# Layer 0 of a four-layer image kernel: one partial sum kept in a PSUM bank, two additions moved from VectorE to GpSimd

## The chip, the cores and the metric

The kernel runs as one launch on one core of a Trainium2 chip. The metric is the device time of a launch in microseconds (us), the median of the runs shown. The engines are named as the profile names them: PE is TensorE, PEld its weight loads, DVE is VectorE, ACT is ScalarE, POOL is GpSimd, and SP is SyncE, which here only issues DMAs.

## The reference, cut to what matters

The input is a tensor of 2 images x 64 channels x 256 x 256 pixels, float32. Four residual layers follow one another; each normalises its input in groups of channels first. The change touches layer 0 alone:

```python
x = x + layer0(_gn(x), img, w_pos, w_img, w_comp)   # then layers 1 (state-space scan), 2 (patch FFT + conv), 3 (block DCT)

def layer0(inp, ...):
    em = concat([w_img @ resized(img), w_pos @ positions])        # 64 channels
    un_em, un_fea = _unfold3x3(em), _unfold3x3(inp)               # 3x3 neighbours, 2 pixels apart
    feature_score = einsum('bckhw,bchw->bkhw', un_em, em)         # em of the neighbour . em of the pixel
    comp_score = sigmoid(einsum('bckhw,c->bkhw', un_fea, w_comp)) # belongs to the neighbour alone
    return einsum('bckhw,bkhw->bchw', un_fea, comp_score * feature_score)
```

Every pixel gets nine terms: its own and those of eight neighbours. The feature score of two pixels is the same from both ends, so that a kernel has to compute it for four directions only.

## The kernel before, in words

The two images with their 64 channels fill the 128 partitions. Layer 0 works on pairs of rows: a **step** `n` is two rows of 256 pixels, a tile of 128 x 512 float32[...]. There are 128 steps, and blocks of eight rows (`R`, four steps, `per`) are loaded by DMA. The loop variable `t` runs over 133 iterations and skews the work: in iteration `t` the embedding of step `t` is made, the products of step `t-2`, the scores and terms of step `n = t-3`, and the sum and the output of step `last = t-4`. The order of every engine's queue is the order of the program (`manual_schedule` names all five engines)[...].

Per iteration, each engine does this, in this order:

- **PE**, eleven matmuls: `pl` (L318) and `pe` (L320) in `embed`; then `score` (L360) of the square `sq`, `score` A, `out` A (L403), `score` B, `out` C, `score` C, `out` D, `score` D, `out` B. A `score` multiplies a tile of products with a block matrix: it sums the 64 channels of an image and puts the sum on all its partitions, in a bank `pf`. The `out` matmuls multiply with the identity and add the four terms of `last` in the bank `acc`.
- **ACT**: `sg` (sigmoid of `pl`), `e` (two halves, from `pe`), `fea` (normalised rows of step `t+1`), `sq` (L352).
- **POOL**: the addition of B for `last` (L380); four products of `e` with its shifted self (`pr`, L355); `gated`, the tile `g` = `fea` x `sg` (L333).
- **DVE**: `mult` "c" (L365), the pixel's own term, from `g` (SBUF) and `pf` (PSUM) into a tile of SBUF; then for each of the four directions `mult` (the neighbour's `g` times the score, for the pixel) and `move` (L370, the pixel's `g` times the score, for the neighbour, into the padded tiles `mvA` to `mvD`); additions (L380) between them; at last `yt` = `xt` + `acc` (L438) and the statistics of `yt` (L439). SP then issues the store of `yt` (L440).

The directions A, B, C, D are the shifts (0, 2), (2, -2), (2, 0), (2, 2) in rows and columns. `moved_to(n, name)` is the view of a moved tile as the receiving pixel sees it: for A that of the same step, for B, C and D that of the step before. After one step the term A holds A + own + moved A, C holds C + moved C, D holds D + moved D, all three added on DVE, and B + moved B is added on POOL an iteration later.

[...] one each for `pl`, `pe` and `acc`, five for `pf`. `acc` has only one bank, so `out` A of an iteration has to wait until `yt` of the iteration before has read it. `pr` has eight buffers (two steps), `term` ten, `fea`, `sg`, `sq` and `yt` two each.

Of the kernel before, what the change touches and what calls it, by code (L numbers as in the profile page):

```python
# [10 lines left out]
F32 = mybir.dt.float32  # L11
BF16 = mybir.dt.bfloat16
AF = mybir.ActivationFunctionType
ALU = mybir.AluOpType
PSUM = bass.MemoryType.PSUM
DRAM = bass.MemoryType.DRAM

P = 128
# [102 lines left out]
class Kernel:  # L121
# [115 lines left out]
    def layer0(self, x, y, coeffs):  # L237
# [3 lines left out]
        nc, tc, a = self.nc, self.tc, self.a  # L241
# [8 lines left out]
        with ExitStack() as ctx:  # L250
# [39 lines left out]

            p_l = ctx.enter_context(tc.tile_pool(name="l0pl", bufs=1, space=PSUM))
            p_e = ctx.enter_context(tc.tile_pool(name="l0pe", bufs=1, space=PSUM))
            p_f = ctx.enter_context(tc.tile_pool(name="l0pf", bufs=5, space=PSUM))
            p_o = ctx.enter_context(tc.tile_pool(name="l0po", bufs=1, space=PSUM))

            xt, fea, sq, pr, term = {}, {}, {}, {}, {}
            inner = slice(2, 2 + W)

            def load(k):
                if 0 <= k < nblk:  # L300
                    xt[k] = pool.tile([P, R, W], F32, name="xt", bufs=3)
                    nc.sync.dma_start(xt[k], xv[:, R * k : R * k + R])
                    nc.sync.dma_start(rts[k % 2][32:38], rv[:, R * k : R * k + R])

            def features(n):
                k, s = divmod(n, per)
                fea[n] = pool.tile([P, 2, W], F32, name="fea")
                self.affine(fea[n], xt[k][:, 2 * s : 2 * s + 2], coeffs)

            def embed(n):  # L310
                k, s = divmod(n, per)
                g, e = gs[k % 2], es[k % 2]
                rows = slice(4 + 2 * s, 6 + 2 * s)
                if s == 0 and k:
                    for t in (gs, es):
                        nc.scalar.copy(t[k % 2][:, 2:4], t[1 - k % 2][:, R + 2 : R + 4])
                pl = p_l.tile([P, 2, W], F32, name="pl")
                nc.tensor.matmul(pl, wcomp, fea[n], start=True, stop=True)  # L318
                pe = p_e.tile([P, 2, W], F32, name="pe")
                nc.tensor.matmul(  # L320
                    pe, w_e, rts[k % 2][:, 2 * s : 2 * s + 2], start=True, stop=True
                )
                sg = pool.tile([P, 2, W], F32, name="sg")
                nc.scalar.activation(sg, pl, AF.Sigmoid)
                for i in range(2):
                    r = 2 * n + i
                    nc.scalar.activation(
                        e[:, 4 + 2 * s + i, inner],
                        pe[:, i],
                        AF.Identity,  # L330
                        bias=by_row[:, r : r + 1],
                    )
                return lambda: nc.gpsimd.tensor_tensor(  # L333
                    g[:, rows, inner], fea.pop(n), sg, ALU.mult
                )

            def at(n):

                k, s = divmod(n, per)
                if s == per - 1 and k + 1 < nblk:  # L340
                    return gs[(k + 1) % 2], es[(k + 1) % 2], 2
                return gs[k % 2], es[k % 2], 4 + 2 * s

            def near(t, j, name):
                dy, dx = shift[name]
                return t[:, j + dy : j + dy + 2, 2 + dx : 2 + dx + W]

            def products(n):
                _, e, j = at(n)
                own = e[:, j : j + 2, inner]  # L350
                sq[n] = pool.tile([P, 2, W], F32, name="sq")
                nc.scalar.activation(sq[n], own, AF.Square)  # L352
                for name in "ABCD":
                    t = pool.tile([P, 2, W], F32, name="pr", bufs=8)
                    nc.gpsimd.tensor_tensor(t, own, near(e, j, name), ALU.mult)  # L355
                    pr[n, name] = t

            def score(t):
                pf = p_f.tile([P, 2, W], F32, name="pf")
                nc.tensor.matmul(pf, self.block, t, start=True, stop=True)  # L360
                return pf

            def mult(n, name, in_, pf):
                t = pool.tile([P, 2, W], F32, name="term", bufs=10)
                nc.vector.tensor_tensor(t, in_, pf, ALU.mult)  # L365
                term[n, name] = t

            def move(n, name, own, pf):
                t = moved[name][n % len(moved[name])]
                nc.vector.tensor_tensor(t[:, :, inner], own, pf, ALU.mult)  # L370

            def moved_to(n, name):

                dy, dx = shift[name]
                n -= dy // 2
                return moved[name][n % len(moved[name])][:, :, 2 - dx : 2 - dx + W]

            def add(eng, n, name, other):
                t = term[n, name]
                eng.tensor_add(t, t, other)  # L380
# [4 lines left out]
            with tc.manual_schedule(engines={E.PE, E.DVE, E.Activation, E.Pool, E.SP}):  # L385
                features(0)
                for t in range(nstep + 5):
                    if t and t % per == 0:
                        load(t // per + 1)
                    gated = embed(t) if t < nstep else None  # L390
                    if t + 1 < nstep:
                        features(t + 1)

                    n, last = t - 3, t - 4
                    acc = None
                    if 0 <= last < nstep:
                        acc = p_o.tile([P, 2, W], F32, name="acc")
                        if last:
                            add(nc.gpsimd, last, "B", moved_to(last, "B"))

                    def out(name):
                        if acc is not None:
                            nc.tensor.matmul(  # L403
                                acc,
                                self.ident,
                                term.pop((last, name)),
                                start=name == "A",
                                stop=name == "B",
                            )

                    if 0 <= t - 2 < nstep:
                        products(t - 2)
                    if gated:
                        gated()
                    if 0 <= n < nstep:
                        g, _, j = at(n)
                        own = g[:, j : j + 2, inner]
                        pf = score(sq.pop(n))
                        mult(n, "c", own, pf)
                        for i, name in enumerate("ABCD"):  # L420
                            pf = score(pr.pop((n, name)))
                            out("ACDB"[i])
                            mult(n, name, near(g, j, name), pf)
                            if name == "A" or n + 1 < nstep:
                                move(n, name, own, pf)
                            if name == "A":
                                add(nc.vector, n, "A", term.pop((n, "c")))
                            if name == "B":
                                add(nc.vector, n, "A", moved_to(n, "A"))
                            if name in "CD" and n:  # L430
                                add(nc.vector, n, name, moved_to(n, name))
                    else:
                        for name in "ACDB":
                            out(name)
                    if acc is not None:
                        k, s = divmod(last, per)
                        yt = pool.tile([P, 2, W], F32, name="yt")
                        nc.vector.tensor_add(yt, xt[k][:, 2 * s : 2 * s + 2], acc)  # L438
                        nc.vector.bn_stats(stats[:, last, :], yt.rearrange("p r w -> p (r w)"))  # L439
                        nc.sync.dma_start(yv[:, 2 * last : 2 * last + 2], yt)  # L440
# [874 lines left out]
```

## Time and profile before

| | |
|---|---|
| median of 3 runs | 19872.43 us (19870.87 to 19875.25) |
| the profiled execution, its own time | 19870.25 us |
| its span, first to last instruction | 19868.5 us |
| layer 0's loop of steps in the span | about 190 to 1666 us |
| layer 1 with its two scans | about 1676 to 16000 us |
| layers 2 and 3 | from about 16000 us |
| DVE busy, whole span / 300 to 1500 us | 95% / over 99% |
| POOL busy, whole span / 400 to 1400 us | 80% / 71 to 72% |
| one step of layer 0 | 11.45 us |

The times come from the hardware profiler on one execution. Busy is the time in which an engine had at least one instruction under way. Instructions of DVE, POOL and PE are pipelined: the next begins a little before the end of the one before it, so the distance between two starts, and not the duration, is what an instruction costs its queue. A matmul of float32 stands as two records ("x2"). The step time is the distance between the same instruction in two neighbouring steps, for instance `yt` at 909.28 and 920.73 us.

### The profile page before, as it was taken

To read this page: it belongs to the slowest core of one execution; us is meant where nothing else is said; L and a number is where in the kernel's file an instruction comes from. 1 tells how busy PE (TensorE), PEld (TensorE's weight loads), DVE (VectorE), ACT (ScalarE), POOL (GpSimd) and SP (SyncE) were. 2 spreads that over 40 slices of the span, in tenths; PEclk is the share of its full clock that TensorE was granted. 3 is DMA by queue.
4 is the path that set the end of the run, shared out by engine and by line. 5 is a ranking of instruction groups with operands and counts; after the bars stand their busy time and mean duration, and the time that the engine had idled before them with its cause. 6 is when DMAs were issued, how large, how long until landed. Compare 5 with 4: busy or idle time off the path is not lost. (4 is left out here: it accounts for less than half of the span.)

```text
span 19868.5 us, 162340 instructions
## 1 busy us (share of the span) xinstructions
PE 14671.3 (74%) x48720; PEld 4849.2 (24%) x48720; DVE 18868.2 (95%) x16476; ACT 11805.5 (59%) x16810; POOL 15933.1 (80%) x7816
## 2 busy tenths in 40 slices
PE   6886777677767767677677767677777688888886
PEld 3332111111111111111111111111111144444444
DVE  7998999999999999999999999999999989999997
ACT  1224666666666666666666666666666655555554
POOL 4776888888888888888888888888888855555554
PEclk9997666666666666666666666666666689989998
DMA  3114666666666666666666666666666500000003
GB/s 118 47 46 110 152 152 153 151 154 150 155 148 157 147 157 147 157 148 156 149 154 151 153 152 153 152 153 151 152 151 152 136 29 29 29 29 29 29 27 144
DMA packets 662179, 2438.82 MB, mean 123 GB/s; under 512 B 131888, under 2 KB 201264, under 8 KB 450160
## 3 DMA queue, kind: packets, MB, share of 16 engines
q1 hardware_dynamic: 661296, 2428.43, 50.9%
q8 instruction: 385, 6.31, 0.1%
q14 instruction: 498, 4.08, 0.1%
HBM read 1990.14 MB, written 437.78 MB: 122 GB/s over the span
## 5 line engine op out<-in xcount | busy, mean ns | idle before, releaser
L792 DVE TENSOR_TENSOR_SCAN h<-da,st,h 128x512 f32<-128x512 f32 x8192 | 9837.4, 1262 | 309.0 <-ACT da L789 223.8
L796 POOL TENSOR_TENSOR h<-h,cb 128x2048 f32<-128x2048 f32 x2048 | 9255.6, 4519 | 166.0 <-POOL st L795 1.5
L789 ACT ACTIVATE da<-dl,p_a 128x512 f32<-128x512 f32 x8192 | 5564.8, 688 | 3985.3 <-DVE h L792 3892.6
L561 PE MATMUL py<-h,t_c_quad 128*32 128x512 f32 x16384 | 3254.7, 817 | 1656.9 <-POOL h L796 1655.9
L561 PE MATMUL pb<-bc,t_c_sel 64*128 64x512 f32 x3072 | 2696.9, 972 | 2379.9 <-DVE h L773 2374.3
L773 DVE TENSOR_TENSOR h<-dv,pb 128x2048 f32<-128x2048 f32 x1536 | 3470.5, 2259 | 40.2 <-DMA dv<-d_dv 40.2
L1021 POOL TENSOR_TENSOR gl<-gl,prod 128x512 f32<-128x512 f32 x1544 | 1961.1, 1271 | 1493.3 <-ACT prod L1017 1417.9
L755 POOL TENSOR_TENSOR h<-dv,cb 128x2048 f32<-128x2048 f32 x512 | 2319.8, 4531 | 16.3 <-DMA dl<-d_dl 16.3
L980 DVE SCALAR_TENSOR_TENSOR acc<-z,tap_b,acc 128x1024 f32<-128x1024 f32 (+1 forms) x1560 | 1987.3, 1274 | 38.8
L561 PEld LDWEIGHTS pb<-bc,t_c_sel 64*128 64x128 f32 x3072 | 661.0, 267 | 4406.4 <-DVE h L773 4339.5
L795 POOL COPY st<-h 128x4 f32<-128x4 f32 x2048 | 387.3, 189 | 1360.1 <-DVE h L792 1329.1
L561 PEld LDWEIGHTS py<-h,t_c_quad 128*32 128x32 f32 x16384 | 423.8, 122 | 3821.8 <-POOL h L796 3225.7
L561 PE MATMUL mm<-xin,p_conv 64*128 64x512 f32 x4096 | 1321.1, 774 | 15.4 <-DMA x1t<-y 15.4
L1064 PE MATMUL pcv<-z,diag 128*128 128x512 f32 x2322 | 1172.0, 622 | 20.4 <-ACT gl L1072 16.6
L1017 ACT ACTIVATE prod<-z,tap_a 128x512 f32<-128x512 f32 x1544 | 1045.0, 714 | 37.6 <-POOL gl L1021 37.4
L949 ACT COPY z<-pz 128x512 f32<-128x512 f32 x768 | 456.8, 599 | 1027.3 <-PE pz L941 924.8
L941 PE MATMUL pz<-t_c_inv,gf 128*128 128x128 f32 (+1 forms) x8192 | 1038.5, 309 | 1.4 <-ACT z L949 1.0
L941 PEld LDWEIGHTS pz<-t_c_inv,gf 128*128 128x128 f32 (+1 forms) x8192 | 848.3, 181 | 517.4 <-issue 311.9
L561 PE MATMUL mm<-u,p_dt 128*128 128x512 f32 x1024 | 931.3, 1064 | 0.0
L561 PE MATMUL py<-u,p_d 128*128 128x512 f32 x1024 | 820.9, 895 | 0.0
L915 PE MATMUL f<-t_w_inT,xf 64*128 64x384 f32 x2048 | 597.0, 615 | 156.4 <-DVE gf L922 155.5
L561 PEld LDWEIGHTS mm<-xin,p_conv 64*128 64x128 f32 x4096 | 459.7, 244 | 982.5 <-issue 982.3
(166 smaller groups left out, 17767.8 us busy)
## 6 DMA issues: line engine op xcount, KB each, us to landing
cb<-d_bc SPq DMA_DIRECT2D x2048, 320.0 KB
dl<-d_dl SPq DMA_DIRECT2D x2048, 256.0 KB
dv<-d_dv SPq DMA_DIRECT2D x2048, 256.0 KB
d_dl<-delta SPq DMA_DIRECT2D x256, 512.0 KB
d_dv<-du SPq DMA_DIRECT2D x256, 512.0 KB
xin<-in_x SPq DMA_DIRECT2D x16, 2048.0 KB
xt<-in_x SPq DMA_DIRECT2D x32, 1024.0 KB
y<-yt SPq DMA_DIRECT2D x128, 256.0 KB
```

Source lines behind the costliest of these rows:

```text
L561: nc.tensor.matmul(out, lhsT, rhs, start=start, stop=stop)
L755: nc.gpsimd.tensor_tensor(h, t["dv", b], t["cb", b][:, 0].unsqueeze(1).to_broadcast([P, 4, T]), ALU.mult,)
L773: nc.vector.tensor_tensor(h, t["dv", b], pb.unsqueeze(1).to_broadcast([P, 4, T]), ALU.mult)
L789: nc.scalar.activation(da, t["dl", b][:, k], AF.Exp, scale=ws[m]["a"][:, k, j : j + 1])
L792: nc.vector.tensor_tensor_scan(h[:, k], da, h[:, k], state[m, b][:, j, k : k + 1], ALU.mult, ALU.add)
L796: nc.gpsimd.tensor_tensor(h, h, t["cb", b][:, 1 + j].unsqueeze(1).to_broadcast([P, 4, T]), ALU.mult)
L915: nc.tensor.matmul(p, x_f[t][half, g], w_in[half], start=True, stop=True)
L941: nc.tensor.matmul(pz[i * n : (i + 1) * n, k, :, 16 * g : 16 * g + 16], gf[t, 2 * e + g, b][:, c0 : c0 + n], inv, start=True, stop=True,)
L980: eng.scalar_tensor_tensor(out, near(s, name, m0, r, k), w, box["t"], ALU.mult, ALU.add)
L1017: nc.scalar.activation(prod, near(s, name, 4 * h + m, n, k), AF.Copy, scale=w)
L1021: nc.gpsimd.tensor_add(acc, acc, prod)
L1064: nc.tensor.matmul(box["t"], diag[:, k], near(s, f"a{i}", 4 * h + m, n, k), start=k == 0, stop=k == 8,)
```

## The change

The own term "c" goes into a bank `part` of a pool of its own instead of an SBUF tile; the pool for it takes one of the five banks of `pf`. DVE adds the term A to it in place, and then adds moved A to it while writing the term A back to SBUF. The additions of moved C and moved D leave DVE: they stand on POOL at the head of the next iteration, ahead of the addition of B, which has been there already, and so ahead of the products and of `gated`. The number of additions on DVE falls from four to two, and on POOL it rises from one to three.

```diff
-            p_f = ctx.enter_context(tc.tile_pool(name="l0pf", bufs=5, space=PSUM))
+            p_f = ctx.enter_context(tc.tile_pool(name="l0pf", bufs=4, space=PSUM))
+            p_s = ctx.enter_context(tc.tile_pool(name="l0ps", bufs=1, space=PSUM))
...
                         if last:
-                            add(nc.gpsimd, last, "B", moved_to(last, "B"))
+                            for name in "CDB":
+                                add(nc.gpsimd, last, name, moved_to(last, name))
...
                         pf = score(sq.pop(n))
-                        mult(n, "c", own, pf)
+                        part = p_s.tile([P, 2, W], F32, name="part")
+                        nc.vector.tensor_tensor(part, own, pf, ALU.mult)
...
                             if name == "A":
-                                add(nc.vector, n, "A", term.pop((n, "c")))
-                            if name == "B":
-                                add(nc.vector, n, "A", moved_to(n, "A"))
-                            if name in "CD" and n:
-                                add(nc.vector, n, name, moved_to(n, name))
+                                nc.vector.tensor_add(part, term[n, name], part)
+                                nc.vector.tensor_add(term[n, name], moved_to(n, name), part)
```

## The prediction, made before the changed kernel had run

> **What bounds the kernel now.** I read the table of stretches first, since the change touches only the first 1,670 us. Columns: length, then busy us of PE, PEld, DVE, ACT, POOL, granted PE clock, DMA share, GB/s.
>
> ```profile
> 300.00:400.00 100.00, 87.92 (x193) 34.34 (x193) 99.69 (x133) 25.62 (x48) 70.72 (x52) 1.00 0.16 57
> ```
>
> DVE has no idle time, PE lacks 12%, POOL 29%. Then the waits from 300 to 1500 us (total, times, longest): who stands still, and for whom?
>
> ```profile
> POOL term L380 <- PE pf L360: 340.6, 105, 3.3
> ...
> PE acc L403 <- DVE yt L438: 139.9, 105, 1.4
> ```
>
> PE waits for DVE once a step, 1.34 us, with `out` A: the only bank `acc` is free when `yt` has read it. POOL is idle 3.25 us a step, ahead of its addition of B; that starts just after DVE's `mult` B of the iteration before ends, so POOL runs one iteration ahead of DVE. DVE is the bound. Its timeline of one step shows what fills it (start, duration):
>
> ```profile
> 902.14 0.68 DVE L370 TENSOR_TENSOR mvB<-g,pf 128x512 f32<-128x512 f32 x1
> 902.74 1.38 DVE L380 TENSOR_TENSOR term<-term,mvA 128x512 f32<-128x512 f32 x1
> 904.04 0.67 DVE L365 TENSOR_TENSOR term<-g,pf 128x512 f32<-128x512 f32 x1
> ...
> 905.24 1.38 DVE L380 TENSOR_TENSOR term<-term,mvC 128x512 f32<-128x512 f32 x1
> 906.54 0.67 DVE L365 TENSOR_TENSOR term<-g,pf 128x512 f32<-128x512 f32 x1
> ...
> 907.74 1.62 DVE L380 TENSOR_TENSOR term<-term,mvD 128x512 f32<-128x512 f32 x1
> 909.28 0.67 DVE L438 TENSOR_TENSOR yt<-xt,acc 128x512 f32<-128x512 f32 x1
> 909.99 0.69 DVE L439 BATCH_NORM_STATS2 stats<-yt 128x6 f32<-128x512 f32 x1
> ```
>
> From start to start an instruction with one input in PSUM takes 0.60. The additions of moved A, C and D, both inputs in SBUF, take 1.30, 1.30 and 1.54. `yt` to the statistics that read it: 0.71, so a result read by the very next instruction costs 0.11 more. POOL at the same time:
>
> ```profile
> 902.30 1.27 POOL L380 TENSOR_TENSOR term<-term,mvB 128x512 f32<-128x512 f32 x1 [3.25 <-PE pf L360]
> 903.53 5.29 POOL L355 TENSOR_TENSOR pr<-e 128x512 f32<-128x512 f32 x4
> 908.78 1.72 POOL L333 TENSOR_TENSOR g<-fea,sg 128x512 f32<-128x512 f32 x1
> ```
>
> The slow additions meet POOL's instructions. At the loop's end POOL has nothing to do, and the same additions cost what the others do, 1650.28 to 1650.88:
>
> ```profile
> 1650.28 0.68 DVE L380 TENSOR_TENSOR term<-term,mvD 128x512 f32<-128x512 f32 x1
> 1650.88 0.67 DVE L438 TENSOR_TENSOR yt<-xt,acc 128x512 f32<-128x512 f32 x1
> ```
>
> [...]
>
> **The change, part by part** (us a step).
>
> DVE before: 5 `mult` and 4 `move` at 0.60 = 5.40; additions 0.60 + 1.30 + 1.30 + 1.54 = 4.74; `yt` 0.71; statistics 0.61. Sum 11.46; the trace has 11.45 (`yt` at 909.28 and 920.73).
>
> DVE after: the additions of C and D go (-2.84). The other two get `part` from PSUM, so that each has one SBUF input [...]: A + own 0.60, then + moved A 0.71, since it reads the result next to it. Sum 5.40 + 1.31 + 0.71 + 0.61 = 8.03. No row shows DVE writing a full tile to PSUM. Three instructions do it or read it back. Bounds: a cheaper write gains nothing, since DVE will no longer set the pace; at the dear end I let each cost as much as a contended addition, 0.70 more: 8.03 + 2.10 = 10.13. I take 0.60: [...] the trace has 0.67 to 0.68 as duration whether an input lies in SBUF or PSUM.
>
> POOL after: three additions at 1.23 (902.30 to 903.53, uncontended) = 3.69. The four products take 5.25 now because two of them wait for DVE; in the fill of the pipeline, with DVE idle, four took 4.32 (191.72 to 196.04) and `g` 1.23. Sum 9.24, against 8.2 plus 3.25 idle. The added wait: D at the head of POOL's queue needs DVE's `mult` D, and behind it are queued B, the products and `g`. C can start when `mult` C ends; PE's scores C and D are 1.72 apart, C itself takes 1.23, so D waits about 0.3: 9.5 in all. No DMA is issued by the moved work, and SP's queue is unchanged.
>
> PE after: the same eleven matmuls. What do they cost when nothing holds them? The fourth iteration, ahead of the first `yt`, shows it:
>
> ```profile
> 207.30 1.02 PE L318 MATMUL pl<-fea,wcomp 128*128 128x512 f32 x2
> 208.26 1.12 PE L320 MATMUL pe<-rt,w_e 38*128 38x512 f32 x2
> ...
> 216.28 1.02 PE L403 MATMUL acc<-term,t_c_ident 128*128 128x512 f32 x2
> 217.14 1.02 PE L318 MATMUL pl<-fea,wcomp 128*128 128x512 f32 x2
> ```
>
> 9.84 from `pl` to `pl`. (Now: 9.84 + 1.34 stall + about 0.27 for the restart = 11.45.) `out` C and `out` D now wait for POOL instead of DVE; `out` B does so already and still starts 0.86 after its neighbour, so a wait that is fulfilled costs nothing.
>
> So the longest queue is PE with **9.84**, then POOL 9.5, DVE 8.03. Do the waits let PE run through? Take iteration t with `pl` at 0; then, with starts 0.86 apart and the spacings 0.96, 1.05 and 0.96 of the first three, `score` A comes at 3.0, `out` A at 3.8, `out` C at 5.6, `score` C at 6.4, `score` D at 8.1, `out` B at 9.0, ready 10.1 (a matmul's result follows its start by 1.02 and a handover of 0.1). DVE: `mult` C ends about 8.6, `mult` D runs 9.3 to 9.9, `move` D to 10.5, `yt` 10.5 to 11.2. `out` A of t+1 is due at 9.84 + 3.8 = 13.6: 2.4 spare. POOL's C runs 8.6 to 9.9, and `out` C of t+1 is due at 15.4: 5.5 spare. The products end at about 17 and are first read in t+2 at 22.7: 5.7 spare. Four banks `pf`: each score takes the bank of four scores earlier; the tightest, `score` D of t+1 at 18.0, needs `mult` "c" of t+1, done at 13.8: 4.2 spare. So I cost the lost bank and PE's new waits at nothing; with that cover gone, each would cost what its wait exceeds it by.
>
> Saving: 11.45 - 9.84 = 1.61 a step. From `pl` at 217.14 to the last `pl` (t = 127) are 122 distances: 196; the first of them took 12.49 instead of 11.45: 1 more. In the last iterations without `pl` and `pe` PE needs less and DVE sets the pace, 8.03 for 11.44 and 10.29, and about 3 in the last: 9. Sum **206**. The profiled execution had 19870.25, 2.2 under the median and so the same within the spread: 19664 from it, 19666 from the median. I take 19665.
>
> **The rivals.**
>
> 1. *DVE or POOL sets the pace at about 10.1 to 10.5.* Place: the three instructions on `part` (10.13, above), or POOL still held back as now: the products and `g` lose 5.25 + 1.72 - 0.45 (the overlap at `g`'s end) - 5.55 = about 1.0 a step to DVE today, which on top of 9.5 gives 10.5. Against it: no DVE instruction of the loop has two SBUF inputs any more. Time: 1.32 to 0.95 saved on some 125 steps, 165 to 119: 19705 to 19751.
>
> 2. *PE's clock falls, and the kernel is slower.* PE would be busy 99% instead of 88% beside a POOL at 95%. With clock c a step is 9.84/c; from c = 0.86 on this is over 11.45. [...] Against it: [...] the clock is 1.00 throughout this loop, the step at 207 to 217 included. For it: from 16000 us on, with PE busy 87%, the clock is only 0.90; that would give 10.93 and still gain 65.
>
> 3. *The change does not do what it says:* PE stays tied to DVE by a wait I have not seen, and the step stays 11.4: no change, 19870.
>
> **How the numbers follow.** PE-paced as worked out: 0.67, 19650 to 19690. Rival 1: 0.20. Rival 3 and small gains: 0.04. Rival 2 and whatever else holds POOL's head so long that the step passes 11.45: 0.09. A measurement of this kernel tells about 0.2%, 40 us, from no change. Faster by more 0.87, within 0.04, slower 0.09. The range takes the first case and most of rival 1: 19645 to 19750.
>
> **What would show it.** Right: `yt` to `yt` at 9.84 between 300 and 1500 us; PE over 98% busy with no wait of `out` A; DVE idle about 1.8 a step, waiting for PE; additions on DVE at 0.68 duration; POOL about 95% busy, `pr` at 1.1 and `g` at 1.27 without the long forms. PE waiting for POOL in `out` C, or DVE durations near 1.3, mean rival 1. A clock under 0.95 in the loop means rival 2. A step over 10.6 makes the prediction wrong.

## The result: 1.0% faster, and the profile after

The changed kernel takes 19667.11 us (median of 4 runs, 19665.71 to 19668.06) against 19873.76 us of the kernel before beside it (the three runs above and one more). The ratio is 0.9896, with a 95% interval from 0.9881 to 0.9911; 206.7 us are saved. The forecast was 19665 us, a saving of 206.

The span of the profiled execution went from 19868.5 to 19665.9 us. Layer 0's loop, from the first own term on DVE to the last statistics, took 1462.4 us before (203.34 to 1665.72) and takes 1253.3 us now (204.53 to 1457.84): 209.1 less. It starts 1.2 us later, and the layers after it took 5.3 us longer in this execution, in code that the change does not touch. So all of the gain lies in the loop.

The same stretch of the changed kernel (length, then busy us of PE, PEld, DVE, ACT, POOL, granted PE clock, DMA share, GB/s):

```profile
300.00:400.00 100.00, 100.00 (x225) 40.88 (x224) 83.26 (x132) 30.50 (x58) 93.14 (x83) 1.00 0.14 50
```

PE has no idle time left, DVE has 17%, POOL 7%. The bound has moved from DVE to PE, and the clock is still 1.00. The waits from 300 to 1300 us (total, times, longest) have turned round:

```profile
DVE part L422 <- PE pf L361: 123.8, 102, 1.2
...
POOL term L381 <- DVE term L366: 69.7, 203, 0.4
```

DVE now waits for PE at the head of its step, 1.2 us each time, and no line of PE waiting for `yt` exists any more. POOL waits twice a step for DVE's `mult`, for C and for D. The timeline of PE:

```profile
907.15 1.02 PE L319 MATMUL pl<-fea,wcomp 128*128 128x512 f32 x2
...
910.97 1.02 PE L405 MATMUL acc<-term,t_c_ident 128*128 128x512 f32 x2
...
916.98 1.02 PE L319 MATMUL pl<-fea,wcomp 128*128 128x512 f32 x2
```

From `pl` to `pl` are 9.83 us, over 122 steps too: (1418.48 - 218.81) / 122 = 9.83. `out` A at 910.97 follows its neighbour without a stall. On DVE:

```profile
902.54 0.69 DVE L430 TENSOR_TENSOR part<-term,part 128x512 f32<-128x512 f32 x1
903.26 0.69 DVE L431 TENSOR_TENSOR term<-mvA,part 128x512 f32<-128x512 f32 x1
903.87 0.68 DVE L366 TENSOR_TENSOR term<-g,pf 128x512 f32<-128x512 f32 x1
...
907.69 0.68 DVE L438 TENSOR_TENSOR yt<-xt,acc 128x512 f32<-128x512 f32 x1
908.41 0.69 DVE L439 BATCH_NORM_STATS2 stats<-yt 128x6 f32<-128x512 f32 x1
910.32 0.69 DVE L422 TENSOR_TENSOR part<-g,pf 128x512 f32<-128x512 f32 x1 [1.21 <-PE pf L361]
```

Both additions that DVE has kept last 0.69: the first had 0.68 before, the addition of moved A 1.38. In this trace writing a tile to PSUM costs DVE what writing it to SBUF does (0.69 against 0.68 for a multiplication); only the read of `part` right behind its write shows, 902.54 to 903.26, 0.72 instead of 0.60. And on POOL:

```profile
905.83 1.09 POOL L381 TENSOR_TENSOR term<-term,mvC 128x512 f32<-128x512 f32 x1 [0.28 <-DVE term L366]
907.32 1.27 POOL L381 TENSOR_TENSOR term<-term,mvD 128x512 f32<-128x512 f32 x1 [0.41 <-DVE term L366]
908.55 1.26 POOL L381 TENSOR_TENSOR term<-term,mvB 128x512 f32<-128x512 f32 x1
909.77 4.38 POOL L356 TENSOR_TENSOR pr<-e 128x512 f32<-128x512 f32 x4
914.10 1.29 POOL L334 TENSOR_TENSOR g<-fea,sg 128x512 f32<-128x512 f32 x1
```

The four products take 4.33 from start to start instead of 5.25 and `g` lasts 1.29 instead of 1.72: POOL lost about 1.4 us a step before, and loses none now. That it lost them to DVE's additions is what the experiments below test.

### The profile page after: what moved, and what is told of

Read it like the earlier page. It is cut to its first block, busy times and chain, and to the rows that moved or that the text cites. A ratio compares the mean times of both kernels' runs of the same rounds, so it can differ in the third digit from the quotient of the medians.

```text
span 19665.9 us, 162715 instructions
## 1 busy us (share of the span) xinstructions
PE 14640.5 (74%) x48720; PEld 4861.7 (25%) x48720; DVE 18472.7 (94%) x16222; ACT 11804.0 (60%) x16810; POOL 16050.1 (82%) x8070
```

## The experiments

My theory: two gains, each enough to speed up DVE. An addition with an input in PSUM is not slowed by POOL: in the kernel before, DVE's multiplications, with one input in PSUM, took 0.60 from start to start, and its additions of moved A, C and D, both inputs in SBUF, 1.30 to 1.54 beside a POOL at work. This contention is called the lock below; in that trace the addition of moved A ended at 904.12, 0.55 after POOL's addition of B (903.57). And two additions leave DVE; then PE's eleven matmuls set the pace. The rivals: only the number of instructions on DVE counts; the single bank `acc` ties PE to DVE; a wait or POOL sets the new pace. Each ratio below is to the kernel before, run beside the experiment: 19867.23 us for the first four, 19872.84 us for the others.

### Each half alone

**The PSUM sum alone:** C and D stay on DVE.

```diff
-                            for name in "CDB":
-                                add(nc.gpsimd, last, name, moved_to(last, name))
+                            add(nc.gpsimd, last, "B", moved_to(last, "B"))
...
                                 nc.vector.tensor_add(term[n, name], moved_to(n, name), part)
+                            if name in "CD" and n:
+                                add(nc.vector, n, name, moved_to(n, name))
```

> The partial sum in PSUM alone; moved C and moved D are still added on DVE. Theory (two separate gains: the lock on SBUF is gone where an input lies in PSUM, and two additions leave DVE): DVE keeps the pace with 5.40 + 1.31 + 1.30 + 1.30 to 1.54 + 0.71 + 0.61 = 10.6 to 10.9 a step, 19765 to 19795 us; the addition of moved A drops from 1.38 to 0.69 in duration, those of C and D stay at 1.3 to 1.6. Rival (the gain is only the two instructions that leave DVE): 11.45 a step, 19873. Rival (the PSUM sum alone brings it all): 9.84 a step, 19667.

Measured: 19768.24 us, ratio 0.9950 (0.9935 to 0.9965). Its DVE timeline:

```profile
908.40 0.69 DVE L430 TENSOR_TENSOR term<-mvA,part 128x512 f32<-128x512 f32 x1
...
911.40 1.19 DVE L381 TENSOR_TENSOR term<-term,mvC 128x512 f32<-128x512 f32 x1
...
913.70 1.62 DVE L381 TENSOR_TENSOR term<-term,mvD 128x512 f32<-128x512 f32 x1
915.25 0.67 DVE L439 TENSOR_TENSOR yt<-xt,acc 128x512 f32<-128x512 f32 x1
```

The step is 10.67 (`yt` at 904.58 and 915.25). The addition with an input in PSUM is short, those with both in SBUF are long, in one and the same step with the same number of instructions as before. Both rivals fall: the place of an input alone is worth 0.78 a step. Of this, 0.57 lies in the two additions with `part`, which now take 0.72 and 0.61 from start to start instead of 0.60 and 1.30. Most of the rest is the addition of moved C, which meets POOL at another moment and lasts 1.19, below the 1.3 to 1.6 of my expectation.

**The move alone:** C and D on POOL, `part` in SBUF.

```diff
-            p_s = ctx.enter_context(tc.tile_pool(name="l0ps", bufs=1, space=PSUM))
+            p_s = ctx.enter_context(tc.tile_pool(name="l0ps", bufs=2))
```

> C and D are added on POOL as in the changed kernel, but the own term and its sum stay in SBUF, so that DVE's two additions have both inputs in SBUF. Theory (lock): each of them meets POOL, lasts 1.3 to 1.6 instead of 0.69, and holds POOL up by 0.4 to 0.6; POOL has 0.69 idle a step, so it becomes the bound at 10.1 to 10.5 a step: 19700 to 19750 us. Rival (only the two instructions that leave DVE count): 9.84 a step, 19667.

Measured: 19676.38 us, ratio 0.9905 (0.9888 to 0.9921), faster than I expected. DVE's two additions first, then POOL's step:

```profile
908.49 1.67 DVE L430 TENSOR_TENSOR part<-term,part 128x512 f32<-128x512 f32 x1
910.20 1.64 DVE L431 TENSOR_TENSOR term<-mvA,part 128x512 f32<-128x512 f32 x1
```

```profile
907.31 1.08 POOL L381 TENSOR_TENSOR term<-term,mvC 128x512 f32<-128x512 f32 x1
908.35 1.26 POOL L381 TENSOR_TENSOR term<-term,mvD 128x512 f32<-128x512 f32 x1
909.58 1.71 POOL L381 TENSOR_TENSOR term<-term,mvB 128x512 f32<-128x512 f32 x1
911.25 4.83 POOL L356 TENSOR_TENSOR pr<-e 128x512 f32<-128x512 f32 x4
916.04 1.26 POOL L334 TENSOR_TENSOR g<-fea,sg 128x512 f32<-128x512 f32 x1
917.27 1.08 POOL L381 TENSOR_TENSOR term<-term,mvC 128x512 f32<-128x512 f32 x1
```

The contention is as expected: both additions are over 1.6 long and end 0.55 after POOL's additions of D and B (910.16 after 909.61, 911.84 after 911.29); one holds up B (1.71 instead of 1.26), the other a product (the four take 4.83 instead of 4.38), and POOL has no idle time. The step is 9.96, so in time the run lies nearer to the rival than to my range; it is the long durations that speak against the rival. DVE's queue has no gap here either, because its two additions last 1.67 and 1.64, so this run alone does not tell which of the two engines sets the pace. The size was off: POOL loses 0.90, as I had said, but undisturbed it needs 9.96 - 0.90 = 9.06 and not 9.24, and the waits for `mult` C and D are gone. So beside the move the PSUM sum adds only the last 0.1 a step, 12.6 us over the 122 distances from `pl` to `pl` (1212.22 here, 1199.67 in the changed kernel). The halves save 0.78 and 1.49 a step alone, and 1.62 together.

### What held the kernel before

**A second accumulator:** four score banks instead of five, and two banks for `acc`.

```diff
-            p_f = ctx.enter_context(tc.tile_pool(name="l0pf", bufs=5, space=PSUM))
+            p_f = ctx.enter_context(tc.tile_pool(name="l0pf", bufs=4, space=PSUM))
-            p_o = ctx.enter_context(tc.tile_pool(name="l0po", bufs=1, space=PSUM))
+            p_o = ctx.enter_context(tc.tile_pool(name="l0po", bufs=2, space=PSUM))
```

> The kernel before with four score banks instead of five, and the free bank given to a second accumulator. Theory (DVE is the bound, the wait of out A for yt is only its echo, and the fifth bank did nothing): PE no longer waits in out A but elsewhere for DVE, the step stays 11.45, 19873 us within 10. Rival (the single accumulator ties PE to DVE and costs the 1.34 a step): 9.84 to 10.1 a step, 19667 to 19700. Rival (the fifth bank matters): over 19885.

Measured: 19865.02 us, ratio 0.9999 (0.9991 to 1.0008): no change. In its waits from 300 to 1300 us PE stands still elsewhere, ahead of a `score`, until a multiplication on DVE is done:

```profile
PE pf L360 <- DVE term L365: 76.4, 87, 0.9
```

`yt` to `yt` is 11.43, and DVE is busy for 996.98 of the 1000 us. PE's wait in `out` A was an echo of a busy DVE. That the fifth score bank did nothing is not shown by itself, since both edits were made together; but DVE is full in both kernels, so neither edit had any time to win or to lose.

**POOL without its products:** `pr` is made in the first step only.

```diff
-                    t = pool.tile([P, 2, W], F32, name="pr", bufs=8)
-                    nc.gpsimd.tensor_tensor(t, own, near(e, j, name), ALU.mult)
-                    pr[n, name] = t
+                    if n == 0:
+                        once[name] = keep.tile([P, 2, W], F32, name=f"pr{name}", tag=f"pr{name}")
+                        nc.gpsimd.tensor_tensor(once[name], own, near(e, j, name), ALU.mult)
+                    pr[n, name] = once[name]
```

> The kernel before with POOL's four products computed in the first step only and those of the first step scored in all steps; DVE, PE and ACT do all they did. Theory (DVE's additions of 1.30 to 1.54 are slow only because POOL is reading SBUF): at most the one that meets the addition of B or g stays slow, DVE needs 9.1 to 9.8, PE sets the pace at 9.84 to 10.0: 19667 to 19690 us. Rival (an addition of two SBUF tiles is slow by itself): 11.45 a step, 19873.

Measured: 19668.38 us, ratio 0.9900 (0.9885 to 0.9915). The same three additions as before the change, both inputs in SBUF:

```profile
914.83 1.38 DVE L381 TENSOR_TENSOR term<-term,mvA 128x512 f32<-128x512 f32 x1
...
917.33 0.68 DVE L381 TENSOR_TENSOR term<-term,mvC 128x512 f32<-128x512 f32 x1
...
919.12 0.68 DVE L381 TENSOR_TENSOR term<-term,mvD 128x512 f32<-128x512 f32 x1
```

C and D cost 0.68 where POOL is silent; that of moved A still meets POOL's addition of B (914.39 to 915.65), ends 0.56 after it and is still 1.38. An addition of two SBUF tiles is not slow by itself here; POOL at work beside it makes it so, and what in POOL's work does it, the run does not tell. The kernel before has the same contrast inside each step: its first addition, A + own, has both inputs in SBUF too, but runs while POOL stands idle (its next instruction begins at 902.30):

```profile
900.95 0.68 DVE L380 TENSOR_TENSOR term<-term 128x512 f32<-128x512 f32 x1
```

The step of 9.83 without the products says less: DVE's sum, 9.8, and PE's happen to be equal here.

### What holds the changed kernel

**One matmul less on PE:** direction C is left out of the sum.

```diff
-                            for name in "CDB":
+                            for name in "DB":
...
-                        if acc is not None:
+                        if acc is not None and name != "C":
```

> The changed kernel with direction C left out of the sum: its addition on POOL and its out matmul are not issued, all else is. Theory (PE's own work sets the pace): ten matmuls, 9.84 - 0.86 = 8.98 a step, still over POOL (8.0 and a wait) and DVE (8.03): 19560 us within 10. Rival (a wait holds the step, not PE's work): 9.84, 19667. Rival (POOL's head, waiting for mult D, sets it): 9.5, 19625.

Measured: 19560.26 us, ratio 0.9843 (0.9827 to 0.9860). On PE:

```profile
898.70 1.02 PE L319 MATMUL pl<-fea,wcomp 128*128 128x512 f32 x2
...
907.68 1.02 PE L319 MATMUL pl<-fea,wcomp 128*128 128x512 f32 x2
```

`pl` to `pl` is 8.98, and so is `yt` to `yt`. The step loses 0.85, and the matmul that is gone had taken 0.86 from start to start, so PE's work is the pace. POOL's addition of C is gone as well, but the run with one product more, below, shows that POOL had time to spare.

**Two instructions more on DVE**, each 0.60, ahead of `yt`:

```diff
+            extra = [keep.tile([P, 2, W], F32, name=f"xx{i}", tag=f"xx{i}") for i in range(2)]
...
+                        for i in range(2):
+                            nc.vector.tensor_tensor(extra[i], own, pf, ALU.mult)
```

> The changed kernel with two more multiplications on DVE in each step, own times score D into a tile nobody reads, ahead of yt. Theory (DVE has 1.8 to spare): DVE 8.03 + 1.20 = 9.23, the step stays 9.84, 19667 us within 8. Rival (PE still follows DVE through yt and out A): 1.2 more a step, 19817.

Measured: 19673.28 us, ratio 0.9900 (0.9885 to 0.9915), and 9.83 a step (`yt` at 899.41, 909.24 and 919.08). DVE's slack is there. The 6 us over the changed kernel lie at the end: the 122 distances from `pl` to `pl` take 1199.66, as in the changed kernel (1199.67), and what follows the last `pl` takes 46.1 instead of 39.4. There DVE sets the pace, and a step is 9.22 instead of 8.02; 2.2 of the difference are a late start of the very last statistics, whose cause stays open.

**One product more on POOL:**

```diff
+            extra = keep.tile([P, 2, W], F32, name="xx", tag="xx")
...
+                nc.gpsimd.tensor_tensor(extra, own, near(e, j, "A"), ALU.mult)
```

> The changed kernel with a fifth product on POOL in each step into a tile nobody reads. Theory (POOL is next in line with 9.14 busy and 0.69 idle): 9.14 + 1.08 = 10.2, and up to 0.3 of the wait for mult D: 10.2 to 10.5 a step, 19712 to 19750 us. Rival (POOL runs an iteration ahead and is not on the path): 19667.

Measured: 19696.72 us, ratio 0.9912 (0.9897 to 0.9927), below the range of the theory and above the rival. In its timeline of POOL:

```profile
908.78 1.17 POOL L358 TENSOR_TENSOR xx<-e 128x512 f32<-128x512 f32 x1
909.78 1.40 POOL L334 TENSOR_TENSOR g<-fea,sg 128x512 f32<-128x512 f32 x1
...
918.86 1.16 POOL L358 TENSOR_TENSOR xx<-e 128x512 f32<-128x512 f32 x1
```

POOL sets the pace at 10.08 a step (908.78 to 918.86) without idle time, while DVE waits 1.21 a step for PE. POOL is next in line, with 0.78 to spare: the extra product takes 1.00, and 9.06 + 1.00 = 10.06. My expectation failed in the load of POOL, as with the move alone: it counted a wait that a late engine does not have, and priced the product at 1.08.

### A version that is faster than both

DVE had 1.8 to spare and PE none, so the sum of C goes to DVE as well: moved C and the term C are added into `part`, and `out` C and POOL's addition of C are dropped. Nothing is left out.

```diff
-                            for name in "CDB":
+                            for name in "DB":
...
-                        if acc is not None:
+                        if acc is not None and name != "C":
...
                                 nc.vector.tensor_add(part, term[n, name], part)
-                                nc.vector.tensor_add(term[n, name], moved_to(n, name), part)
+                            if name == "B":
+                                nc.vector.tensor_add(part, moved_to(n, "A"), part)
+                            if name == "C":
+                                c = term.pop((n, "C"))
+                                if n:
+                                    nc.vector.tensor_add(part, moved_to(n, "C"), part)
+                            if name == "D":
+                                nc.vector.tensor_add(term[n, "A"], c, part)
```

> A further step on from the changed kernel: moved C and the term C are added into the same PSUM sum on DVE (moved C after move C, the term last, after move D), so that out C on PE and the addition of C on POOL are gone and nothing is left out. Theory: DVE 9 x 0.60 + 4 x 0.60 + 0.71 + 0.61 = 9.12, PE 8.98, POOL 8.0 and a wait; the step is 9.12 to 9.25, 19577 to 19593 us. Rival (the longer chain through PSUM on DVE delays out A or yt): 9.84 or more, 19667 or more.

Measured: 19582.75 us, ratio to the kernel before 0.9854 (0.9840 to 0.9869), 84 us under the changed kernel. The stretch from 300 to 1300 us:

```profile
300.00:1300.00 1000.00, 1000.00 (x2202) 390.38 (x2200) 996.19 (x1652) 317.37 (x604) 888.22 (x771) 1.00 0.17 59
```

`yt` to `yt` is 9.09 (902.51 and 911.60). DVE has no gap and sets the pace, and PE is right behind it, with ten matmuls that took 8.98 in the run without C; only POOL (89% busy) and ACT (32%) have time left.

## Why the prediction was right

- **What bounded the kernel before.** Right: DVE, through its additions. The second accumulator showed that PE's stall was only an echo; the runs without products and with the PSUM sum alone showed from two sides that the additions were slow because of POOL. The additions last 0.69 with `part` in PSUM against 1.64 to 1.68 with `part` in SBUF. Ahead of the runs, that an input in PSUM would free an addition was the author's estimate, from the 0.60 of the multiplications that had one.
- **DVE after, 8.03.** Right: from start to start the waits for PE take 1.30 ahead of `part` (908.41 to 910.32 less 0.61), 0.26 ahead of `mult` A and 0.23 ahead of `mult` D; 9.83 less these is 8.04. The dear end for a write to PSUM, 0.70 more, did not come: the duration is 0.69. The 0.60 from start to start that was taken for it was the author's estimate, from durations of 0.67 to 0.68 in the trace of the kernel before, none of them of a write to PSUM.
- **PE after, 9.84.** Right: 9.83, and the run without C moved it by one matmul. The lost score bank and PE's new waits cost nothing. The handover of 0.1 after a matmul was an estimate; ahead of `part` it is 0.04 (the `score` of `sq` starts at 909.15 and lasts 1.13, `part` starts at 910.32).
- **POOL after, 9.5.** Right in rank, off in size. Undisturbed it needs 9.06 and not 9.24, because moved C costs 1.04 from start to start (908.35 less 907.31 in the move alone) and not 1.23. The wait for `mult` D was put at 0.3, while the figures beside it, 1.72 less 1.23, give 0.49; the trace has 0.41 there and 0.28 ahead of C, and neither is part of POOL's load. What POOL lost to DVE before was put at 1.0 and came out at 1.4: 0.92 in the products and 0.43 in `g`, where the prediction took 0.45 off. The price of rival 1 for POOL, 10.5, was too high all the same, because of the 9.5 in it; with two contending additions left (the move alone) a step is 9.96.
- **The sum.** That 19665 met 19667 is luck in part. The 122 distances from `pl` to `pl` lost 196.3 (1395.98 to 1199.67), and 197 had been forecast. The end of the loop lost more than the 9 of the forecast: from the last `pl` on it took 52.60 before and takes 39.36 now, 13.2 less. In the kernel before, `yt` had fallen 4.6 behind `pl` there (0.55 now), and the sum left out that lag. The start of the loop gave 0.5 back. In the profiled executions the loop lost 209.1 and the rest of the kernel took 6.5 more; the medians differ by 206.7.
- **PE's clock, the rival on the slower side.** It was 1.00 in the changed kernel from 210 us to the loop's end at 1458, with PE busy all the time up to 1450. A step of 9.84/c was an estimate; in the kernel before a matmul lasts 2.07 to 2.08 from 190 to 200 us, at a clock of 0.50, and 1.02 in the loop at 1.00. That the clock would stay under 0.86 in this loop, as it must for a slower kernel, was not shown by any trace. "1.00 throughout this loop", said of the kernel before, was not quite so: it was 0.76 from 200 to 210 us and 0.83 from 1640 to 1650.

## What to carry to other kernels

Where DVE and GpSimd both work on SBUF tiles all the time, look at the durations of DVE's instructions with two SBUF inputs: if they are about twice those of the others, as here (1.38 to 1.62 against 0.68), put one input in PSUM (1.38 became 0.69 here) or move the instruction, and count the time that GpSimd gets back too (about 1.4 a step here). Then add up every engine's step from starts, undisturbed, because the longest of these sums is what the kernel fell to here; a step measured where nothing had yet stalled, in the fill of the pipeline, gave PE's to 0.01. Waits of an engine that is early, as POOL's 0.28 and 0.41 here, are no part of its load. And two remedies for one bound need not add up once the next engine stands in the way: here 0.78 and 1.49 gave 1.62.

## What the runs showed that I had not expected

On POOL, instructions of one size and type have two prices in these traces. In the changed kernel the additions of moved D and moved B and the tile `g` last 1.27, and the addition of moved C 1.09. Of the four products of a step, in the order A, B, C, D, the third lasts 1.27 too and the others 1.03 to 1.09 (from 899.94 on: 1.03, 1.09, 1.27, 1.09). In the code, the two inputs of each long one start at the same column of their tiles (`g`, moved D, product C) or four columns apart (moved B); those of each short one start two columns apart. This is a pattern found in one program, not a cause: no run shifted a view to try it, and the profile does not tell where the tiles themselves begin.
